# Unread transposes at the waits of block 1, step lists of their own for the first two units, and five instead of four leading pairs in block 3

## The chip, the cores and the metric

The kernel runs on one core of one Trainium2 chip. A core has five engines that run side by side, each with its own queue of instructions: PE (matrix products and transposes), DVE (vector operations), ACT (activation functions and copies), POOL (GpSimd, elementwise work here) and SP, which only issues transfers here. The metric is the device time of one execution in microseconds (us). A span in the profile begins with the first recorded instruction, and all positions below are microseconds from there.

PE has a clock that a throttle grants. The profile shows it as a share of full speed. In this trace it is either 1.00 or 0.50, and it changes only at the ends of windows of 3.413 us, so a position such as "the window 1002.41 to 1005.82" below means one of these.

## The reference, cut to what matters

The activations are 4 sequences of 256 tokens with 512 features, 1024 tokens in all. Two layers run one after the other, each made of a mixer and a feed-forward part, each with a layer norm ahead of it and a residual sum behind it:

```python
x = x + _L0_attn_ref(_layernorm(x), ...)   # block 1: retention, 32 heads of 128, 8 key/value heads
x = x + _L0_ffn_ref(_layernorm(x), ...)    # block 2: router, top 8 of 64, adds a mix of biases
x = x + _L1_attn_ref(_layernorm(x), ...)   # block 3: state space mixer, 128 heads of 64, 8 groups
x = x + _L1_ffn_ref(_layernorm(x), ...)    # block 4: top 16 of 64 low-rank adapters
```

Block 1, for each head and in chunks of 128 tokens:

```python
q = rope(h @ Wq.T); k = rope(h @ Wk.T); v = h @ Wv.T
G = cumsum(softplus(h @ Win.T + dt_bias) * -exp(A_log_bias))
scores = (q @ k.T) * where(causal, exp(G[i] - G[j]), 0)
y = scores @ (v * dt) + (carried state of the earlier chunk)
y = y / rms(y) * gnorm_w * silu(h @ Wg.T)
out = y @ Wo.T
```

Block 3 has the same shape with other parts: a projection to x, B and C, a causal convolution over 4 tokens with a silu behind it, products of C, B and a decay matrix for each head, a gate, an RMS norm within each of the 8 groups, and an output projection.

## The kernel before, in words

The tokens lie in 8 tiles of 128 (`k.x[0]` to `k.x[7]`), and are worked on in two halves of 4 tiles, which are 512 columns for PE. The normalised activations lie in `k.xs[half]` with features on the partitions, split into a rounded high part and the remainder: `xs_hi`, `xs_lo`. Every weight is split in the same way when it has been loaded (`split`, L140 on ACT for the high part, L145 on POOL for the low part), and a product is hi·hi + lo·hi + hi·lo. A projection (`proj`, L206) is thus 12 matmuls of 128x512, which take some 4.7 us at full clock.

`Weights` (L151 to L191) holds all weight pieces of the kernel in one list in order of use; a piece is 512 KB. `until(n)` splits all pieces up to the n-th and issues the loads of the next two; there are two raw buffers, so a load waits until the piece two places ahead has been split. `step` (W in the lists) splits one more piece if the position `due` allows; in block 1 `due` is -1, so W does nothing there. Pieces whose index is in `LATE` keep their place in program order on ACT. In all other things each engine's order is made by a scheduler from its own estimates of durations, under the dependencies and under extra order constraints: `k.line` fixes the order of PE instructions between steps, and `k.behind(a, b)` puts a behind b without a wait for data.

Block 1 (`retention`, L310 to L593) works in 32 units, each a key/value group, a pair of heads and a half. For each unit one of three lists of steps is followed: `FIRST1` for unit 0, `STEP1` for most, `SIDE1` while side work is pending. The letters: Q queries of the next unit (projection and rotation), K keys, values and transposed values of a next group, G gates (projection), S scores (L408, and L412 on DVE, which multiplies the decay matrix `m` with the scores), A attend and square (L420, L438), U silu, N the norm's transposes (L445) and the gate's product (L448), D decays of the next unit (L299 on POOL or DVE, L303, then exponentials), F and C the output projection of a unit (`finish`, L464, with the weight `wo`), P side work. One unit's `wo` is split by the first call of `u.w.o()`, that is in F, which stands in the next unit's list.

Ahead of unit 0 the layer norm of both halves runs tile by tile (`moments` L86 on DVE, a power on POOL, `centre` L101, transposes by `turned` L109, high part on ACT, low part L127 on DVE), mixed with the first keys, the time steps and the first gates.

Near the end of block 1, half 0's residual is finished before half 1's, and its share of the router (block 2) and of block 3's preparation begins as side work in the units that remain.

Block 3 (`state_space`, L672 to L980) works in 64 units: 8 groups by 4 head pairs by 2 halves. In the list `order` (L899) the first entry is a range whose pairs are all done for half 0 first and then for half 1; after that each pair is done for half 0 and at once for half 1, with the same weights in place; the last two pairs are again done half by half. Where two units of a pair don't follow each other, the weights (`wx`, `wg`, `wo`, and `wbc` for the first pair of a group) are loaded and split once for each half. With `FIRST3 = 1` and `NC = 8` the first range has 1·8//2 = 4 pairs, 0_0 to 0_3. Half 1 can start only once its residual, router and preparation are done; until then `while after.half not in ready` pumps side work, among it the running sums `ps_cum` (L255) that need `e` (L251).

Of the kernel before, what the change touches and what calls it, by code (L numbers as in the profile page):

```python
# [11 lines left out]
F32 = mybir.dt.float32  # L12
F32R = mybir.dt.float32r
AF = mybir.ActivationFunctionType
ALU = mybir.AluOpType
# [3 lines left out]
P = 128  # L19
NB, SEQ, HID = 4, 256, 512  # L20
NT = NB * SEQ // P
KC = HID // P
HT = NT // 2
# [1 line left out]
EPS = 1e-5  # L25
GONE = -30000.0
YB = 3
LONE1, FIRST3, LONE3 = 3, 1, 2
PUMP = 1
AHEAD = 0  # L30
BANK1, BANK3 = "o", "x"
LATE = (0, 3)
FIRST1 = "U S0 S1 S2 K Q0 W Q1 K A0 A1 W K G0 N0 W G1 N1 D E W".split()
STEP1 = "S0 D F S1 S2 K Q0 W Q1 K A0 A1 U W K C W P G0 N0 W G1 N1 E P W".split()
SIDE1 = "S0 D F P S1 S2 T K Q0 P W Q1 T K A0 A1 U W K C P P W G0 P N0 W G1 N1 E P W".split()
STEP3 = "W T0 T1 B I0 W M0 M1 X0 X1 I1 O0 G0 W W O1 W W P O2 W W G1 P W O3 D0 D1 W W".split()
FILL3 = "B X0 X1 I0 I1 P P G0 G1 W W P P W D0 D1 E E".split()
# [44 lines left out]
def moments(k, tc, t, tag):  # L82

    nc = tc.nc
    stats = k.small([P, 6], f"stats_{tag}_{t}", "ln_stats")
    nc.vector.bn_stats(stats, k.x[t])  # L86
    mv = k.small([P, 2], f"mv_{tag}_{t}", "ln_mv", 6)
    nc.vector.bn_aggr(mv, stats)
    rstd = k.small([P, 1], f"rstd_{tag}_{t}", "ln_rstd", 6)
    nc.gpsimd.tensor_scalar_add(rstd, mv[:, 1:2], EPS)  # L90
    one = nc.gpsimd.tensor_tensor(rstd, rstd, k.neghalf[:, 0:1], ALU.pow)
    if tag == "4" and t == HT - 1:
        k.rooted = one
    return mv[:, 0:1], rstd
# [10 lines left out]
def turned(k, tc, xn, name):  # L105

    ps = k.psum.tile([P, KC, P], F32, tag=k.bank, name=f"ps_{name}")
    for c in range(KC):
        k.line(tc.nc.tensor.transpose(ps[:, c, :], xn[:, c * P:(c + 1) * P], k.ident))  # L109
    return ps  # L110


def normalize(k, tc, half, tag, into=("xn",)):


    nc = tc.nc
    tiles = [HT * half + at for at in range(HT)]
    of = [moments(k, tc, t, tag) for t in tiles]
    ahead = len(into)
    xns = [centre(k, tc, tiles[at], of[at], tag, into[at]) for at in range(ahead)]  # L120
    yield
    for at, t in enumerate(tiles):
        xn = xns[at]
        ps = turned(k, tc, xn, f"xn_{tag}_{t}")
        hi, lo = (part[:, :, at * P:at * P + P] for part in k.xs[half])
        nc.scalar.copy(hi, ps)
        nc.vector.tensor_tensor(lo, ps, hi.bitcast(F32), ALU.subtract)  # L127
        if at + ahead < HT:
            xns.append(centre(k, tc, tiles[at + ahead], of[at + ahead], tag, into[at % ahead]))
        yield  # L130
# [179 lines left out]
def retention(k, tc, io, arrive, begun, done, tail):  # L310
# [3 lines left out]
    nc = tc.nc  # L314
    NH, NG = 32, 8
    with ExitStack() as st:
# [5 lines left out]
        n = 2 * NH * 2  # L322
# [29 lines left out]
        def rope(ps, hi, lo, name):  # L352
# [3 lines left out]
            if name == "k_0_0":  # L356

                tc.keep_in_program_order(one)
            t2 = k.wk.tile([P, 2, SEQ], F32, tag="xd", name=f"r2_{name}")
            nc.vector.tensor_tensor(t2[0:64], ps[64:128], mid(sin[64:128], 2), ALU.mult)  # L360
            nc.vector.tensor_tensor(t2[64:128], ps[0:64], mid(sin[0:64], 2), ALU.mult)  # L361
            nc.gpsimd.tensor_tensor(t1, t1, t2, ALU.add)  # L362
            t1 = t1.rearrange("p b s -> p (b s)")
            nc.scalar.copy(hi, t1)
            nc.vector.tensor_tensor(lo, t1, hi.bitcast(F32), ALU.subtract)

        def keys(g, half, w):

# [30 lines left out]
        def scores(u, blk):  # L399

            kh, kl = u.kk
            zj, zi = ((0, 0), (1, 1), (0, 1))[blk]
            ps = k.psum.tile([P, 4, P], F32, tag="y", name=f"ps_sc_{u.name}_{blk}")
            for b in range(2):
                aj = slice((2 * b + zj) * P, (2 * b + zj) * P + P)
                ai = slice((2 * b + zi) * P, (2 * b + zi) * P + P)
                for i, (a, q) in enumerate(((kh, 0), (kh, 1), (kl, 0))):
                    k.line(nc.tensor.matmul(  # L408
                        ps[:, b::2, :], a[:, aj], qs[:, q, :, ai], start=(i == 0), stop=(i == 2)
                    ))  # L410
            m = u.m[:, blk]
            nc.vector.tensor_tensor(m, m, ps, ALU.mult)  # L412

        def attend(u, z):
            blocks = (((0, 0),), ((0, 2), (1, 1)))[z]
            nm = f"{u.name}_{z}"
            ps = k.psum.tile([P, 4, P], F32, tag="g", name=f"ps_y1_{nm}")
            for q in range(4):
                for i, (zj, blk) in enumerate(blocks):
                    k.line(nc.tensor.matmul(  # L420
# [19 lines left out]
        def norm(u, z):  # L440

            nm = f"{u.name}_{z}"
            ps_t = k.psum.tile([P, 4, P], F32, tag="y", name=f"ps_yt1_{nm}")
            for q in range(4):
                k.line(nc.tensor.transpose(ps_t[:, q, :], u.yr[z][:, q, :], k.ident))  # L445
            r = k.wk.tile([P, 4, P], F32, tag="yh", name=f"r1_{nm}", bufs=YB)
# [62 lines left out]
        for i in range(-1, len(units) + 1):  # L509
# [50 lines left out]
            def value(z):  # L560
# [111 lines left out]
def state_space(k, tc, io):  # L672
# [461 lines left out]
def tile_two_layers(ctx: ExitStack, tc: tile.TileContext, io: dict, out: bass.AP):  # L1134
# [47 lines left out]
    def line(ins):  # L1182
# [5 lines left out]
        k.front = []  # L1188
        k.done = ins

    k.act, k.small, k.pump, k.behind, k.line = act, small, pump, order, line
    k.n, k.follow, k.done, k.main, k.root = 0, None, None, None, None
    k.rooted = None
    k.front = []
    k.hold = k.scaled = k.turned = None
    k.const = ctx.enter_context(tc.tile_pool(name="const", bufs=1))
    k.smalls = ctx.enter_context(tc.tile_pool(name="smalls", bufs=3))
    k.dram = ctx.enter_context(tc.tile_pool(name="dram", bufs=1, space=bass.MemoryType.DRAM))
# [110 lines left out]
```

## Time and profile before

| what | value |
|---|---|
| median of 3 runs | 2536.8 us (2534.87 to 2537.2) |
| the profiled execution | 2536.5 us, of which the span is 2534.7 us |
| mean granted clock of PE | 0.987 |
| PE busy | 2425.6 us, 96% of the span, 14000 matmuls and transposes |
| DVE, POOL, ACT busy | 2062.1, 1597.8, 1473.0 us (81%, 63%, 58%) |
| DMA | 206.25 MB, 81 GB/s on average |

The profiled execution is 0.3 us below the median of the runs, so a saving can be taken from the one or the other. The 36875 instructions of the trace are grouped by their line in the kernel. Durations are those of the records; in the slices of the page each digit is a share in tenths. In the views by window the columns are the stretch and its length, then busy time and number of instructions of PE, PE's weight loads, DVE, ACT and POOL, then the granted clock, the mean busy share of the DMA engines and GB/s. In the timelines the columns are start, duration, engine, line, operation, output and inputs, shape, the number of instructions taken together, and in brackets how long the engine stood idle ahead of it and what ended the wait. Idle time in PE sums to 109 us (2534.7 − 2425.6).

### The profile page before, as it was taken

The numbers are of one execution on the slowest core, as the hardware profiler recorded it, in microseconds if no ns is written. First come the engines' busy times: TensorE is split into PE (matmuls) and PEld (weight loads), VectorE is DVE, ScalarE is ACT, GpSimd is POOL, SyncE is SP. The second block draws the span as 40 slices with busy tenths as digits, with TensorE's granted clock in tenths as the row PEclk, the third lists the DMA queues.
The fourth block names the chain that finished last, engine by engine and source line by source line (L and its number), as shares of the span: only waits on it lengthen the run. The fifth ranks groups of instructions, "written<-read, shape, count | busy, mean of one in ns | idle before, by whom it ended". The sixth has DMA issues, their size and how long they took to land.

```text
span 2534.7 us, 36875 instructions
## 1 busy us (share of the span) xinstructions
PE 2425.6 (96%) x14000; PEld 2008.6 (79%) x14000; DVE 2062.1 (81%) x2629; ACT 1473.0 (58%) x2363; POOL 1597.8 (63%) x1123
## 2 busy tenths in 40 slices
PE   7899999999999897899999999999999999999989
PEld 6688888888887775678878888888888888888767
DVE  6577677778888769697988988988988988979973
ACT  3555555556655455465766756666756657657631
POOL 4555546557766547485874865856756855857840
PEclk9899999999999998999999999999999999999999
DMA  3312212213332222332232323222323223323221
GB/s 108 77 58 67 57 44 67 68 50 100 92 92 63 88 77 69 96 117 76 84 92 69 107 67 92 92 76 84 100 67 100 84 67 96 95 69 108 82 90 69
DMA packets 82896, 206.25 MB, mean 81 GB/s; under 512 B 8672, under 2 KB 10592, under 8 KB 82720
## 3 DMA queue, kind: packets, MB, share of 16 engines
q1 hardware_dynamic: 82720, 203.90, 26.5%
q8 instruction: 111, 1.82, 0.3%
q14 instruction: 65, 0.53, 0.1%
HBM read 200.86 MB, written 3.01 MB: 80 GB/s over the span
## 4 chain that ended last, share of the span: by engine, by line
PE 37%; DVE 15%; POOL 6%; issue 4%; ACT 3%; DMA 1%; POOLq 0%; SPq 0%; ACTq 0%; DVEq 0%
PE ps_x L206 9%; PE ps_g L206 8%; PE ps_o L877 8%; DVE m L773 4%; PE ps_y L821 4%; DVE conv L732 3%; PE ps_bc L206 3%; DVE yl L840 2%; PE ps_o L1122 2%; POOL xs L835 1%; DVE m L299 1%; POOL sqs L849 1%; PE ps_t L796 1%; PE ps_h L206 1%; ACT m L1160 1%
## 5 line engine op out<-in xcount | busy, mean ns | idle before, releaser
L206 PE MATMUL ps_g<-xs_hi,wg_h 128*128 128x512 f32 x768 | 306.4, 399 | 2.3 <-ACT wg_h L140 1.7
L773 DVE TENSOR_TENSOR m<-m,cb 128x1536 f32<-128x1536 f32 x128 | 274.7, 2150 | 40.2 <-ACT m L1160 38.8
L206 PE MATMUL ps_g<-xs_lo,wg_h 128*128 128x512 f32 x768 | 300.1, 391 | 0.0
L206 PE MATMUL ps_g<-xs_hi,wg_l 128*128 128x512 f32 x768 | 298.6, 391 | 0.0
L732 DVE SCALAR_TENSOR_TENSOR conv<-ps_x,cw,conv 128x510 f32<-128x510 f32 (+2 forms) x384 | 269.9, 736 | 20.1 <-ACT conv L730 17.5
L1157 ACT ACT_TABLE_LOAD x191 | 245.1, 1283 | 4.1 <-PEq L1297 0.8
L299 POOL TENSOR_TENSOR m<-gb,start 128x512 f32<-128x512 f32 x128 | 151.4, 1185 | 140.6 <-PE ps_y L821 93.0
L877 PE MATMUL ps_o<-wo_h,yh 128*128 128x512 f32 x512 | 213.0, 416 | 20.0 <-DVE acc L885 18.9
L835 POOL TENSOR_TENSOR xs<-xs,sg 128x512 f32<-128x512 f32 x128 | 206.7, 1615 | 38.2 <-DVE xs L831 37.3
L849 POOL TENSOR_TENSOR sqs<-sqs,sq 128x512 f32<-128x512 f32 x112 | 192.9, 1722 | 32.9 <-ACT sq L847 32.9
L362 POOL TENSOR_TENSOR r_q<-r_q,r_q 128x512 f32<-128x512 f32 x64 | 103.3, 1613 | 175.0 <-DVE r_q L361 174.8
L303 POOL TENSOR_SCALAR_AFFINE_SELECT m<-m 128x1024 f32<-128x1024 f32 x160 | 206.0, 1287 | 0.1
L877 PE MATMUL ps_o<-wo_h,yl 128*128 128x512 f32 x512 | 198.2, 401 | 7.8 <-DVE yl L840 7.8
L1160 ACT ACTIVATE xs<-conv,cb 128x512 f32<-128x512 f32 x128 | 90.8, 723 | 193.2 <-DVE conv L732 193.1
L877 PE MATMUL ps_o<-wo_l,yh 128*128 128x512 f32 x512 | 202.7, 396 | 0.0
L206 PE MATMUL ps_x<-xs_lo,wx_h 128*128 128x512 f32 x512 | 202.6, 396 | 0.0
L206 PE MATMUL ps_x<-xs_hi,wx_h 128*128 128x512 f32 x512 | 202.0, 395 | 0.4 <-DVE conv L732 0.2
L206 PE MATMUL ps_x<-xs_hi,wx_l 128*128 128x512 f32 x512 | 201.3, 393 | 0.0
L1160 ACT ACTIVATE m<-m 128x1024 f32<-128x1024 f32 (+1 forms) x160 | 181.5, 1135 | 28.0 <-POOL m L303 28.0
L145 POOL TENSOR_TENSOR wo_l<-raw_wo,wo_h 128x1024 fp32r<-128x1024 f32 x60 | 147.8, 2464 | 79.1 <-ACT wo_h L140 71.8
L145 POOL TENSOR_TENSOR wx_l<-raw_wx,wx_h 128x1024 fp32r<-128x1024 f32 x38 | 96.3, 2534 | 154.3 <-ACT wx_h L140 141.5
L821 PE MATMUL ps_y<-m,xd 128*64 128x128 f32 x2048 | 178.1, 280 | 13.5 <-DVE m L773 9.5
(276 smaller groups left out, 6949.1 us busy)
## 6 DMA issues: line engine op xcount, KB each, us to landing
gb<-cum SPq DMA_DIRECT2D x160, 512.0 KB
raw_wx<-in_L_attn_in_x_dram SPq DMA_DIRECT2D x38, 512.0 KB
raw_wg<-in_L_attn_in_gate_dram SPq DMA_DIRECT2D x38, 512.0 KB
raw_wo<-n_L_attn_out_proj_w_dram SPq DMA_DIRECT2D x38, 512.0 KB
raw_wq<-in_L_attn_Wq_dram SPq DMA_DIRECT2D x22, 512.0 KB
raw_wg<-in_L_attn_Wg_dram SPq DMA_DIRECT2D x22, 512.0 KB
raw_wo<-in_L_attn_Wo_dram SPq DMA_DIRECT2D x22, 512.0 KB
raw_wkv<-in_L_kv_dram SPq DMA_DIRECT2D x11, 512.0 KB
```

Source lines behind the costliest of these rows:

```text
L145: low = nc.gpsimd.tensor_tensor(lo, w, hi.bitcast(F32), ALU.subtract)
L206: k.line(tc.nc.tensor.matmul(ps, a[:, c, :], b[:, c, :], start=(c == 0 and n == 0), stop=(c == KC - 1 and n == 2)))
L299: one = engine.tensor_tensor(m[:, blk], gb[:, min(blk, 1)], last(at, P), ALU.add)
L303: nc.gpsimd.affine_select(out=causal, in_=causal, compare_op=ALU.is_ge, fill=GONE, base=0, pattern=[[0, 8], [1, P]], channel_multiplier=-1,)
L732: nc.vector.scalar_tensor_tensor(acc[:, :, j:], ps[:, :, :SEQ - j], cw[:, ch, TAPS - 1 - j:TAPS - j], acc[:, :, j:], ALU.mult, ALU.add,)
L773: made = nc.vector.tensor_tensor(mh, mh, cbs[p.g, p.half].rearrange("p z b l -> p z (b l)").unsqueeze(2) .to_broadcast([P, 3, 2, 2 * P]), ...
L821: one = nc.tensor.matmul(ps_y[h * D:h * D + D, 2 * b + z, :], p.xe[:, n, b, h, :] if blk == 2 else xd[:, 2 * b + zs, h, :], m[:, blk, 2 * ...
L835: nc.gpsimd.tensor_tensor(xs, xs, p.sg[n], ALU.mult)
L849: nc.gpsimd.tensor_tensor(total, total, sq, ALU.add)
L877: own.out = nc.tensor.matmul(ps, y[:, at], w[:, n, :], start=(i == 0), stop=(i == 5))
L1157: load = nc.scalar.preload_act_table_set(table)
L1160: ins = nc.scalar.activation(out, in_, func, bias=bias, scale=scale)
```

## The change: what it does

There are three edits.

First, `k.warm(n, ...)` issues n transposes of the identity into a tile of PSUM that nothing reads, at a fixed place in PE's order. There are 88: 14 behind the first score matmul of unit 0, 8 ahead of the third block of scores of unit 0 and 8 each ahead of the first and third of unit 1, 14 ahead of the transposes of `xn_3_3` (tile 3 of the layer norm of block 3, at the turn from block 1 to block 3), 18 ahead of the last unit's second attend, and 9 ahead of the norm of each of the last two units.

Second, order in block 1. `FIRST1` and `STEP1` lose entries W and get V: in unit 0, V splits all weight pieces up to that unit's `wo`; in unit 1 it splits up to the pieces of the second group's keys; in later units it does nothing. One more index, 7, is kept in program order. In the layer norm, half 1's statistics (`bn_stats`) of a tile are put behind half 0's low part of the tile with the same number ("half 0 first"), and the rotation of the second keys `k_0_1` behind the low part of the rotation before it ("queries first").

Third, `FIRST3` is 5 and counts pairs: half 0 runs 0_0 to 0_3 and 1_0, then half 1 runs the same five, and from 1_1 on each pair is done for both halves. Pair 1_0 is the first of group 1, so four more pieces (`wbc`, `wx`, `wg`, `wo`) are loaded and split once more: four transfers of 512 KB, four casts on ACT and four subtractions on POOL.

```diff
-LONE1, FIRST3, LONE3 = 3, 1, 2
+LONE1, FIRST3, LONE3 = 3, 5, 2
-LATE = (0, 3)
-FIRST1 = "U S0 S1 S2 K Q0 W Q1 K A0 A1 W K G0 N0 W G1 N1 D E W".split()
-STEP1 = "S0 D F S1 S2 K Q0 W Q1 K A0 A1 U W K C W P G0 N0 W G1 N1 E P W".split()
+LATE = (0, 3, 7)
+WARM = {"xn_3_3": 14}
+WARM1 = {(0, 2): ("g", 8), (1, 0): ("g", 8), (1, 2): ("g", 8)}
+FIRST1 = "U S0 S1 S2 K Q0 Q1 K A0 A1 K V G0 N0 G1 N1 D E".split()
+STEP1 = "S0 D F S1 S2 K Q0 W Q1 K A0 A1 V U K C P G0 V1 N0 G1 N1 E P".split()
...
-    nc.vector.bn_stats(stats, k.x[t])
+    one = nc.vector.bn_stats(stats, k.x[t])
+    if tag == "1" and t >= HT:
+        k.behind(one, k.parts[t - HT], "half 0 first")
...
+    if name in WARM:
+        k.warm(WARM[name], into=ps[:, KC - 1, :])
...
-        nc.vector.tensor_tensor(lo, ps, hi.bitcast(F32), ALU.subtract)
+        k.parts[t] = nc.vector.tensor_tensor(lo, ps, hi.bitcast(F32), ALU.subtract)
...
+            if name == "k_0_1":
+                k.behind(one, k.low, "queries first")
...
-            nc.vector.tensor_tensor(lo, t1, hi.bitcast(F32), ALU.subtract)
+            k.low = nc.vector.tensor_tensor(lo, t1, hi.bitcast(F32), ALU.subtract)
...
+            n = units.index(u)
+            if (n, blk) in WARM1:
+                k.warm(WARM1[n, blk][1], WARM1[n, blk][0])
...
+                    if (n, blk, b, i) == (0, 0, 0, 0):
+                        k.warm(14, "g")
...
+            if u is units[-1] and z == 1:
+                k.warm(18, into=ps[:, 3, :])
...
+            if u in units[-2:] and z == 0:
+                k.warm(9, into=ps_t[:, 3, :])
...
+                V=lambda n=0: k.weights.until(u.w.o.n if i == 0 else units[4].w.kv.n - 1 + n if i == 1 else -1),
...
-    order = [range(FIRST3 * NC // 2)]
+    order = [range(FIRST3)]
...
+    def warm(n, tag=None, into=None):
+        if into is None:
+            k.n += 1
+            into = k.psum.tile([P, P], F32, tag=tag, name=f"ps_warm_{k.n}")
+        if k.follow is None:
+            k.follow = k.done
+        for _ in range(n):
+            line(nc.tensor.transpose(into, k.ident, k.ident))
+        k.follow = k.done
```

More of the change, by code (lines that the diff above doesn't have):

```diff
@@ L1189, in line @@
         k.done = ins
+    def warm(n, tag=None, into=None):
[7 more added lines that the diff above has]
+        k.follow = k.done
     k.act, k.small, k.pump, k.behind, k.line = act, small, pump, order, line
+    k.warm = warm
     k.n, k.follow, k.done, k.main, k.root = 0, None, None, None, None
@@ L1195, in tile_two_layers @@
     k.hold = k.scaled = k.turned = None
+    k.parts = {}
     k.const = ctx.enter_context(tc.tile_pool(name="const", bufs=1))
```

## The prediction, made before the changed kernel ran

> **What bounds the kernel now.** I read the stretches by window first: busy time of PE, weight loads, DVE, ACT, POOL, then the clock.
>
> ```profile
> 60.00:80.00 20.00, 15.37 (x89) 12.54 (x87) 12.79 (x19) 11.20 (x28) 12.55 (x11) 0.93 0.33 88
> 80.00:100.00 20.00, 13.35 (x61) 10.86 (x62) 8.02 (x11) 10.44 (x10) 11.31 (x7) 0.72 0.48 127
> ...
> 1000.00:1050.00 50.00, 38.40 (x230) 29.36 (x230) 38.87 (x48) 20.99 (x31) 27.11 (x16) 0.90 0.26 79
> 1400.00:1800.00 400.00, 396.02 (x2459) 325.83 (x2457) 355.82 (x423) 261.41 (x361) 272.75 (x172) 1.00 0.28 85
> ```
>
> In steady block 3 PE is busy 396.02 of 400 us: PE is the bound, nothing is to be had there. The change works where PE idles and its clock falls: 4.6 of 20 us idle at 60 to 80, 6.65 at 80 to 100 with a clock of 0.72, 11.6 of 50 at 1000 to 1050. All of PE's idle time is 109 us. Next PE's timeline, for the waits at those places (in brackets the wait and what ended it).
>
> ```profile
> 53.62 0.58 PE L408 MATMUL ps_sc<-qs,kh 128*128 128x256 f32 x1 [3.71 <-DVE qs L365]
> 76.75 0.51 PE L408 MATMUL ps_sc<-qs,kh 128*128 128x256 f32 x2 [2.37 <-DVE r L448]
> 85.43 1.22 PE L464 MATMUL ps_o<-wo_h,yh 128*128 128x512 f32 x2 [7.54 <-ACT wo_h L140]
> 87.87 0.79 PE L464 MATMUL ps_o<-wo_l,yh 128*128 128x512 f32 x1 [1.22 <-POOL wo_l L145]
> ...
> 842.73 1.11 PE L109 MATMUL ps_xn<-ident,xn 128*128 128x128 f32 x4 [3.14 <-DVE xn L101]
> ...
> 892.24 2.95 PE L420 MATMUL ps_y<-v,m 128*128 128x128 f32 x16 [3.72 <-DVE m L412]
> ...
> 1033.12 2.08 PE L255 MATMUL ps_cum<-upper,e 128*128 128x128 f32 x8 [7.03 <-DVE e L251]
> ```
>
> The longest is for a weight. Its transfer was issued early and its cast came late:
>
> ```profile
> 21.48 0.33 SPq L176 DMA_DIRECT2D raw_wo<-in_L_attn_Wo_dram  x1
> ```
>
> ```profile
> 84.35 1.03 ACT L140 CAST wo_h<-raw_wo 128x1024 fp32r<-128x1024 f32 x1
> ```
>
> So this wait is one of order and not of data: the cast stands in the list of unit 1 and not in that of unit 0. The clock I read in its own windows of 3.41 us, first all of PE, then its transposes alone (those that read the identity).
>
> ```profile
> 1002.41:1005.82 3.41, 1.90 (x18) 1.25 (x14) 3.41 (x6) 1.69 (x2) 3.16 (x4) 1.00 0.44 154
> 1005.82:1009.23 3.41, 2.94 (x11) 2.04 (x10) 3.41 (x6) 3.40 (x7) 3.41 (x3) 0.50 0.00 0
> 1070.66:1074.07 3.41, 1.53 (x24) 1.32 (x24) 3.41 (x4) 3.38 (x5) 0.00 (x0) 1.00 0.56 179
> 1074.07:1077.48 3.41, 3.14 (x14) 2.61 (x15) 3.41 (x4) 3.17 (x5) 2.61 (x2) 1.00 0.33 125
> ```
>
> ```profile
> 1002.41:1005.82 3.41, 1.53 (x10) 1.00 0.44 154
> ```
>
> A window with 1.90 us of PE, 1.53 of it transposes, was followed by half clock; one with 1.53 us and no transpose kept full clock. The clock follows the matmuls, and transposes did not hold it.
>
> **The change part by part.** The profiled execution took 2536.5 us (span 2534.7), 0.3 under the median of 2536.8; the sum is made against 2536.5.
>
> (a) "Half 0 first". On DVE half 1's statistics stand between half 0's low parts: two of 0.69 us ahead of the second low part at 10.46. Put behind them, half 0's last tiles turn some 0.6 us earlier and the first time-step matmul comes at 13.5 and not 14.18: −0.7 (0 to −1.2). The order adds a wait for half 1's statistics: behind them stand their aggregates, POOL's powers and half 1's transposes, which nothing needs before the second time steps.
>
> (b) Unit 0. The second score matmul waits 3.71 us for the low part of the rotated queries; POOL's sum for it (1.6 us) stood behind two decay sums L299 (1.2 each), then came DVE's rotation of k_0_1 (2.1 us). The changed orders put the queries' sum ahead of L299 and that rotation behind. The low part is then ready at about 48.5 and PE at 48.9: the wait goes (−3.71), and with it the drop of the clock at 53.50 to 56.92, of which some 2.4 us are work at half speed (−1.2). The 14 transposes, at 0.0875 us each (4 transposes of the norm take 0.35 from start to start at full clock), now cost their 1.2. The 8 ahead of block 2 lie in the wait for the decays' exponentials, about 1 us. Sum −3.7 (−1.2 if a wait for the second product's other inputs stays, −4.9 if the 14 are covered). The rotation moved back feeds half 1's keys, first needed units later.
>
> (c) Unit 1. `wo`'s cast moves to about 66, behind the squares of unit 0, its subtraction on POOL to 69, into POOL's idle 4.37 us there. The waits of 7.54 and 1.22 go: −8.76. What is late next is `r` (L448): on DVE both decay sums L299, for units 1 and 2, now stand ahead of it, and they wait for their broadcast transfers gb (issued 68.52, landed 75.34). By the shift of (a) and (b) they land near 71, the scores come at 74.0 where the shift alone gives 72.35: +1.65. The third block's scores wait some 0.3 longer for L412. The 12 output matmuls stay at half clock. Sum −6.8 (−3.6 to −9.2: the upper end if the cast waits on ACT as long as the 2.37 us of the row above and the transfers don't come earlier, the lower if the clock holds). Queries of unit 2 start at 82.0 and not 93.17, −11.2 with (a) and (b). The pieces split earlier than before (V, V1) bring transfers and splits forward; POOL is busy 11 of 20 us here.
>
> (d) End of block 1. The 14, 18 and 9 transposes take 1.2, 1.6 and 0.8 us and lie inside waits of 3.14, 3.72, 2.04 and 1.47 us: 0 (up to +3 where such a wait has gone, since the earlier work brings them together). Their clock windows stay at half, by the reading above. Other orders there (the gate's product no longer behind a transfer wait of its queue) give −2, from one wait of 2.04 (0 to −4).
>
> (e) Block 3. Between the last value transposes of half 1's preparation and its running sums PE now has 46 matmuls ready at 0.228 us, 10.5 us, and before 24, 5.5. DVE's chain to `e` (1021.09 to 1033.07) gets three convolutions of 0.74 us between, so `e` comes at about 34.8, and the wait of 7.03 falls to 3.4: −3.6. At half 1's first pair PE waits 1.76 us for `m` and 0.53 for a gate's silu; both stages are now fed by a fifth pair: −2.3. Against that four more pieces: each 512 KB on SP's queue, a cast on ACT of 1.05, a subtraction on POOL of 2.5. DMA engines are 26% busy there, POOL 27 and ACT 21 of 50 us, so they lie beside PE's work; where one is late its user waits. No row shows these splits; the ends are 0 and 4 × 1.76 = 7, and I take +2, nearer to steady block 3, whose 1% idle holds such splits. Net −3.9 (−10, with all waits of the stage gone, to +4).
>
> Sum: −0.7 −3.7 −6.8 −2.0 −3.9 = −17.1: 2519.4, by the median 2519.7.
>
> **The rivals.**
>
> A: the transposes hold the clock. Then (c) runs its 12 output matmuls at full speed (−2.4), the stretch 841.98 to 848.81 its 5.4 us of work at twice the speed (−2.7), and 893.18 to 896.59 too (−1.7): −6.8, 2512.6. For it: waits are filled, and a filled PE otherwise kept its clock. Against it: the window at 1002.41. The Trainium skill, "TensorE: Matmul & The Clock Gate", section "Why this matters for your kernels", says that an idle gap of over some 3 us between bursts of matmuls loses the clock; read as a rule on any PE work it gives this rival. Its section "Part 4: PE-mode transpose" says that transposes don't count as such work; the window at 1002.41 agrees with that one.
>
> B: block 3's part gives nothing: −3.6 stays, the two short waits stay, four pieces cost 7: net +3.4, and the rest −13.2: 2526.7. For it: lone pairs reload all, and DVE is at 3.41 of 3.41 us in both quoted stretches, so `e` can come as late as PE's new work is long. Against it: PE had 11.6 us idle there.
>
> C, slower: the pieces of the fifth pair are split when they are needed, as `wo` was at 84.35, so cast, subtraction and the wait behind lie on the path: 1.05 + 2.5 + 1.76 = 5.3 us, by 4 21.2, 2536.5 − 13.2 + 21.2 = 2544.5. It decides from 13.2 us. For it: it happened in unit 1. Against it: in block 3 W splits ahead of need, and PE idles 1% there.
>
> D: V does not do what it says, and the cast of `wo` stays late: without (c), 2526.2. The cast is an order on ACT that a scheduler decides; in the changed program it stands ahead of unit 1's scores.
>
> **How the numbers follow.** A difference under 0.2%, 5 us, is about what a measurement of this kernel can't tell from none. Chances: the forecast 0.52 (its own range 2513 to 2525), A 0.12, B 0.17, D 0.04; block 3 losing between 8 and 18 us, so that nothing is left, 0.06; C 0.09. Faster 0.85, same 0.06, slower 0.09. The range goes from A with the lower ends of (c) and (d), 2505, to B with the upper ends of (b) and (d), 2531, and leaves out 0.15.
>
> **What would show it.** (a) first time-step matmul at 13.5; (b) no wait of over 1 us before the second score matmul and full clock until about 70; (c) cast of `wo` before 70, queries of unit 2 near 82; (d) the 14 and 18 transposes inside waits that end as before, half clock behind them; (e) the wait for `e` at 3 to 4 us, and no wait of over 2 us for wbc, wx, wg, wo of 1_0. I am wrong if DVE, which now carries more between 60 and 80 and at 1020, becomes what PE waits for, or if the clock falls at new places.

## The result, and the profile after

The changed kernel took 2520.9 us (median of 6 runs, 2515.6 to 2522.3) against 2536.5 of the kernel before: a ratio of 0.9936 with an interval of 0.9923 to 0.9949. A second set on another occasion gave 2519.0 us and 0.9926 (0.9914 to 0.9939). It is faster, by 16 to 17 us; 2519.4 had been forecast (2519.7 by the median). One of the six runs of the kernel with four leading pairs, which is used below, took 4917 us and is left out of its median. The profiled executions are 2536.5 and 2519.2 us, 17.3 apart, and the sum of the prediction was 17.1. The total came out, but the stages show that it did so by terms that missed on both sides.

To compare stages, both traces are cut at the same piece of PE's work: the first matmul of the queries of units 1, 2 and 31 (Q1, Q2, Q31), the first B and C projection of block 3 (BC0), the first time-step projection for its half 1 (DT1), the first B and C projection of group 2 and group 7 (BC2, BC7), the first matmul of the two routing products of block 4 (R0, R1), and the end.

| stage, us | before | after | difference | predicted |
|---|---|---|---|---|
| start to Q1 | 57.6 | 57.6 | +0.1 | −4.4 (a, b) |
| Q1 to Q2 | 35.6 | 26.3 | −9.3 | −6.8 (c) |
| Q2 to Q31 | 760.5 | 761.4 | +0.9 | 0 |
| Q31 to BC0 | 20.9 | 21.3 | +0.4 | (d) |
| BC0 to DT1 | 137.0 | 125.1 | −11.9 | −2.0 (d) |
| DT1 to BC2 | 296.8 | 293.0 | −3.8 | −3.9 (e) |
| BC2 to BC7 | 904.1 | 904.5 | +0.4 | 0 |
| BC7 to R0 | 215.8 | 218.2 | +2.4 | 0 |
| R0 to R1 | 33.5 | 40.4 | +6.9 | 0 |
| R1 to the end | 72.9 | 69.6 | −3.4 | 0 |

How far a stage moves from one execution to the next was seen in a second profiled execution of the changed kernel: Q1 to Q2 was 28.2 there and not 26.3, all others were within 1.1 us. (Other kernels with one and the same order in a stage differ by more in one case, DT1 to BC2, as will be seen.)

The windows that were shown of before, now of after (stretch, length, busy time of PE, weight loads, DVE, ACT, POOL, then clock, DMA share, GB/s):

```profile
60.00:80.00 20.00, 18.44 (x108) 15.24 (x107) 14.16 (x21) 13.57 (x30) 16.47 (x13) 1.00 0.44 128
80.00:100.00 20.00, 18.99 (x108) 16.37 (x107) 13.50 (x19) 12.44 (x26) 13.47 (x13) 1.00 0.23 64
1000.00:1050.00 50.00, 46.97 (x291) 38.24 (x290) 37.95 (x50) 28.79 (x40) 31.81 (x18) 1.00 0.37 105
1400.00:1800.00 400.00, 397.06 (x2473) 327.53 (x2472) 357.47 (x428) 260.88 (x359) 276.95 (x173) 1.00 0.28 85
```

PE is nearly full at 60 to 100 and the clock is 1.00 there; steady block 3 is what it was. PE's waits in the changed kernel, by its timeline (line numbers are those of the changed kernel: L420 is L408 of before, L482 is L464, L466 is L448):

```profile
48.80 1.69 PE L1218 MATMUL ps_warm<-ident 128*128 128x128 f32 x14
51.70 0.38 PE L420 MATMUL ps_sc<-qs,kh 128*128 128x256 f32 x1 [1.21 <-DVE qs L374]
...
56.82 0.50 PE L420 MATMUL ps_sc<-qs,kh 128*128 128x256 f32 x2 [2.23 <-DVE m L426]
...
76.64 0.50 PE L420 MATMUL ps_sc<-qs,kh 128*128 128x256 f32 x2 [1.40 <-DVE r L466]
...
833.58 0.66 PE L116 MATMUL ps_xn<-ident,xn 128*128 128x128 f32 x4 [1.63 <-DVE xn L106]
...
878.65 2.13 PE L1218 MATMUL ps_y<-ident 128*128 128x128 f32 x18
...
1033.84 0.50 PE L896 MATMUL ps_o<-wo_h,yh 128*128 128x512 f32 x1 [2.02 <-ACT yh L858]
...
1191.18 0.69 PE L840 MATMUL ps_y<-m,xd 128*64 128x128 f32 x4 [4.16 <-DVE m L792]
...
2412.59 0.80 PE L213 MATMUL ps_lg<-xs_lo,wr_parts 128*128 128x512 f32 x1 [4.35 <-DVE xs_lo L134]
```

The waits of 7.54 for `wo_h`, 7.03 for `e` and 3.72 for `m` are gone. Three of over 2.1 us are new: 2.23 us at 56.82, on the decays' products; 4.16 us at 1191.18, on block 3's product of the decays with those of C and B, with half clock from 1189.7 to 1196.5; and 4.35 us at 2412.59, on a low part in block 4, far from every edit. What DVE did ahead of the product that PE waits for at 1191.18:

```profile
1181.25 8.12 DVE L910 SCALAR_TENSOR_TENSOR x<-acc,r,x 128x512 f32<-128x512 f32 x4 [2.24 <-POOL r L882]
```

Four residual sums wait 2.24 us for POOL there and end at 1189.37. In the two kernels with four leading pairs DVE's timeline lists no wait ahead of the same four sums, and PE has no wait of over 1 us behind them; in all twelve profiles with five leading pairs PE waits 4.0 to 4.9 us. The cast of `wo` in ACT's timeline stands where the prediction put it, a little later:

```profile
69.29 1.05 ACT L147 CAST wo_h<-raw_wo 128x1024 fp32r<-128x1024 f32 x1
```

### The profile page after: what moved, and what is told of

It is laid out like the page before. It is cut to its first block, busy times and chain, and to the rows that moved or that the text cites. A ratio compares the mean times of both kernels' runs of the same rounds, so it can differ in the third digit from the quotient of the medians.

```text
span 2517.4 us, 37059 instructions
## 1 busy us (share of the span) xinstructions
PE 2430.5 (97%) x14088; PEld 2015.1 (80%) x14088; DVE 2067.6 (82%) x2629; ACT 1476.6 (59%) x2367; POOL 1603.9 (64%) x1127
## 4 chain that ended last, share of the span: by engine, by line
PE 58%; DVE 23%; POOL 8%; ACT 5%; issue 4%; DMA 2%; SPq 0%; POOLq 0%; ACTq 0%; DVEq 0%
PE ps_g L213 11%; PE ps_x L213 7%; PE ps_o L896 7%; PE ps_q L213 6%; PE ps_o L482 6%; DVE conv L751 5%; DVE m L792 5%; PE ps_y L840 3%; PE ps_bc L213 2%; PE ps_sc L420 2%; DVE yl L859 2%; PE ps_y L436 2%; DVE m L306 2%; PE ps_o L1141 2%; ACT m L1179 2%
## 5 line engine op out<-in xcount | busy, mean ns | idle before, releaser
L306 POOL TENSOR_TENSOR m<-gb,start 128x512 f32<-128x512 f32 x128 | 149.5, 1171 | 133.2 <-PE ps_y L840 98.0
L152 POOL TENSOR_TENSOR wo_l<-raw_wo,wo_h 128x1024 fp32r<-128x1024 f32 x61 | 152.8, 2505 | 68.8 <-ACT wo_h L147 67.0
L840 PE MATMUL ps_y<-m,xd 128*64 128x128 f32 x2048 | 178.4, 280 | 14.7 <-DVE m L792 14.1
```

The lines of the kernel that those rows point to most:

```text
L152: low = nc.gpsimd.tensor_tensor(lo, w, hi.bitcast(F32), ALU.subtract)
L306: one = engine.tensor_tensor(m[:, blk], gb[:, min(blk, 1)], last(at, P), ALU.add)
L840: one = nc.tensor.matmul(ps_y[h * D:h * D + D, 2 * b + z, :], p.xe[:, n, b, h, :] if blk == 2 else xd[:, 2 * b + zs, h, :], m[:, blk, 2 * ...
```

## The experiments

All kernels are timed against the kernel before. "Stage" means the cuts of the table above, in one profiled execution each.

**No transposes at all.**

```diff
     def warm(n, tag=None, into=None):
+        if k.follow is None:
+            k.follow = k.done
+        return
```

> The changed kernel without its 88 transposes that nothing reads; all else, also the order of the steps, as in the changed kernel. Stages by the trace of the changed kernel: from the second unit's queries to the third's 26.3 us, from the last unit's queries to the third group's B and C 439.5 us, from the first to the second routing product of block 4 40.4 us. Theory 1, the recorded one (transposes do not hold the clock): the clock stays where it is in the changed kernel, also from 19 to 92 us, the first of these stages stays within 0.5 us of 26.3, the second too. Theory 2 (transposes hold the clock): the clock falls to half near 53 and near 74 us, the first stage is 2 to 4 us longer, and near 880 us, where the 18 and the 9 stood, a window falls as well, 1 to 2 us. Both: here the order on DVE in block 4 has the last low part of half 0 ahead of the four residual sums, as in the kernel before, so the stage of block 4 should go from 40.4 back to 33.5 us, about -7. In all: theory 1 about 2513, theory 2 about 2517 to 2519.

Measured: 2536.1 us, ratio 0.9994 (0.9985 to 1.0004). Without the 88 transposes the whole change is worth nothing. Neither theory had that. Half clock came back at 52.8 to 63.0 and 80.1 to 83.5, and Q1 to Q2 took 28.6 us, as theory 2 said, and R0 to R1 went back to 34.2. But the large loss was elsewhere: BC0 to DT1 took 137.7 and not 125.1 us, although only 27 of the transposes stand in that stage, all in its first 20 us (in the changed kernel 18 at 878.65 and 9 at 885.17). The orders of the two programs show why that can be: without the transposes the scheduler puts DVE, ACT, POOL and PE into another order from the end of block 1 into block 3. The transposes are all that was taken out.

**Four leading pairs.**

```diff
-LONE1, FIRST3, LONE3 = 3, 5, 2
+LONE1, FIRST3, LONE3 = 3, 4, 2
```

> The changed kernel with four leading pairs in block 3, as before. The recorded prediction puts the fifth pair at -3.9 us, so the stage from the last unit's queries to the third group's B and C goes from 439.5 to about 443.5 us. The rival, read from the two traces (this stage fell by 15.2 us in all): the fifth pair is worth 8 to 14 us, and the stage comes out at 448 to 453 with the wait of about 7 us for e back. In both the order on DVE in block 4 is again that of the kernel before, so the block 4 stage goes from 40.4 to about 33.5. In all: prediction about 2516, rival 2521 to 2526.

Measured: 2515.8 us (median of five runs), 0.9913 (0.9895 to 0.9931). DT1 to BC2 is 296.1 and not 293.0: the fifth pair is worth 3.1 us in its own stage in this pair of executions, near the 3.9 predicted, and the rival of 8 to 14 falls. BC0 to DT1 is 125.3, so the large gain there isn't the fifth pair's. And R0 to R1 is 33.1, BC7 to the end 321.7 where the changed kernel has 328.1: the kernel with four pairs is not slower as a whole, because the changed kernel loses 6.4 us in block 4.

**The lists of before.**

```diff
-LATE = (0, 3, 7)
+LATE = (0, 3)
-FIRST1 = "U S0 S1 S2 K Q0 Q1 K A0 A1 K V G0 N0 G1 N1 D E".split()
-STEP1 = "S0 D F S1 S2 K Q0 W Q1 K A0 A1 V U K C P G0 V1 N0 G1 N1 E P".split()
+FIRST1 = "U S0 S1 S2 K Q0 W Q1 K A0 A1 W K G0 N0 W G1 N1 D E W".split()
+STEP1 = "S0 D F S1 S2 K Q0 W Q1 K A0 A1 U W K C W P G0 N0 W G1 N1 E P W".split()
```

> The changed kernel with the step lists of block 1 and the kept places of the kernel before (no V, wo of unit 0 is split in unit 1's list). Recorded prediction: V is worth 6.8 us, and the wait of about 7.5 us before the first output product comes back, so the stage from the second unit's queries to the third's goes from 26.3 to about 33. Rival: V is worth all of the 9.3 us that this stage gained, 35.6. If the transposes hold the clock through the wait it ends nearer 33 with full clock at 80 us, if not nearer 36 with half clock. Block 3 and block 4 as in the changed kernel: 2526 to 2529 in all.

Measured: 2528.8 us, 0.9968 (0.9957 to 0.9980). Q1 to Q2 is 35.1 us, 8.8 more, and the wait is back, with half clock from 79.5 to 89.7; PE's timeline of this run:

```profile
83.59 1.22 PE L482 MATMUL ps_o<-wo_h,yh 128*128 128x512 f32 x2 [7.72 <-ACT wo_h L147]
86.02 0.80 PE L482 MATMUL ps_o<-wo_l,yh 128*128 128x512 f32 x1 [1.21 <-POOL wo_l L152]
```

So the lists carry nearly all of (c); the 8 transposes ahead of the scores (at 73.94) don't bridge a wait of that length.

**The low part ahead of the residual sums in block 4.**

```diff
         if (p.g, p.half) == (NG - 1, 0):
             k.behind(one, own.made, "products first")
+        if (p.g, p.half) == (NG - 1, 1):
+            k.behind(one, k.parts[HT - 1], "low part first")
```

> The changed kernel with one more order on DVE: in block 4 the four residual sums of half 1 stand behind the last low part of half 0's layer norm, as they do by chance in the kernel before. Theory: this order alone cost the changed kernel the 4.35 us wait before the second routing product and the half clock behind it, so the stage between the two routing products goes from 40.4 to about 33.5 us, and the time to about 2513. Rival: the sums that move back make half 1 later by as much, the end gains less than 2 us: 2518 to 2520.

Measured: 2514.5 us, 0.9911 (0.9897 to 0.9926); R0 to R1 is 35.4 and not 40.4. DVE in the changed kernel:

```profile
2407.07 4.86 DVE L910 SCALAR_TENSOR_TENSOR x<-acc,r,x 128x512 f32<-128x512 f32 x4 [1.13 <-POOL r L882]
2411.86 0.68 DVE L134 TENSOR_TENSOR xs_lo<-ps_xn,xs_hi 128x512 fp32r<-128x512 f32 x1
```

and with the added order:

```profile
2407.53 0.69 DVE L134 TENSOR_TENSOR xs_lo<-ps_xn,xs_hi 128x512 fp32r<-128x512 f32 x1 [1.81 <-ACT xs_hi L133]
2408.13 3.88 DVE L910 SCALAR_TENSOR_TENSOR x<-acc,r,x 128x512 f32<-128x512 f32 x4
```

Four sums that wait 1.13 us for POOL and then run 4.86 us stood ahead of the one low part that PE needed. In the kernel before the low part came first (at 2427.07, the sums at 2429.78). The order was the scheduler's, not the edit's.

**Early transposes out.**

```diff
-WARM1 = {(0, 2): ("g", 8), (1, 0): ("g", 8), (1, 2): ("g", 8)}
+WARM1 = {}
-                    if (n, blk, b, i) == (0, 0, 0, 0):
-                        k.warm(14, "g")
```

> The changed kernel without the 14 and the three times 8 unread transposes of units 0 and 1; the 41 at the end of block 1 stay, and up to about 835 us every engine's order is that of the changed kernel. Theory 2 (transposes hold the clock): half clock appears between 50 and 90 us, as in the kernel without any of the 88, and the stage from the second unit's queries to the third's is 28 to 29 us where the changed kernel has 26.3. Theory 1 (they do not): no half clock there, 26.3 us or a little less. The stage from the last unit's queries to the third group's B and C should stay near 439.5 us, since its transposes are in place; should it go to 455, the early ones act through the schedule of what comes later.

Measured: 2518.7 us, 0.9937 (0.9922 to 0.9952), no difference to the changed kernel that can be told. Half clock did appear, from 54.6 to 61.4, and the third unit's queries begin at 86.7 us, against 83.9 and 86.4 in the two executions of the changed kernel; Q1 to Q2 is 27.2, short of what theory 2 expected. Over all runs, the third unit's queries begin at 86.7 and 87.2 us in the two kernels without these transposes (this one and the first experiment) and at 83.9 to 86.4, mean 85.2, in seven executions with them and an otherwise equal front: 1 to 2 us, which the total is too coarse to show. It isn't there any more where the last unit's queries begin: Q31 is at 845.4 us in this run, and at 845.4 and 846.9 in the two executions of the changed kernel.

**Late transposes out, and the orders pinned.** Three runs separate the transposes from the order that they bring about. First the 41 at the end of block 1 are left out and the scheduler is free:

```diff
-WARM = {"xn_3_3": 14}
+WARM = {}
...
-            if u is units[-1] and z == 1:
-                k.warm(18, into=ps[:, 3, :])
...
-            if u in units[-2:] and z == 0:
-                k.warm(9, into=ps_t[:, 3, :])
```

> The changed kernel without the 41 unread transposes at the end of block 1 (14, 18, 9, 9); the scheduler, which counts them in its own timeline, then also orders the engines in another way from the end of block 1 into block 3. The stage from the last unit's queries to the third group's B and C was 439.5 us with all 88 and 456.4 with none, so about 455 is expected by every theory; if it stays at 440, the early 38 were the cause.

Then, for the two others, each engine's instructions from there into block 3 are chained in a given order, without waits for data (`PINS` lists their places; `late_off` with the places of the changed kernel, the changed kernel with the places of `late_off`):

```diff
+def pin(k, tc):
+    ...
+    for engine, runs in PINS.items():
+        for run in runs:
+            for first, then in zip(run, run[1:]):
+                tc.add_manual_dep(
+                    by[engine][then], by[engine][first].name,
+                    mybir.DependencyInfo(mybir.DependencyClass.NoSync, mybir.DependencyReason.DATA),
+                    reason="pinned",
+                )
...
         of.run4()
+        pin(k, tc)
```

> No transposes at the end of block 1, as in the run above, but PE, DVE, ACT, POOL and SP are pinned to the order that they have in the changed kernel from there into block 3. Theory A (the transposes' gain there is an accident of the schedule: they move the scheduler's estimates, and it orders DVE, ACT and POOL better): the stage stays at 439 to 442 us. Theory B (they hold PE's clock, or fill it, in the waits): about 452 to 456 us.

> The counterpart: the changed kernel with all its transposes, but all engines from the end of block 1 into block 3 pinned to the order that the scheduler makes when the 41 are not there. Theory A: the stage from the last unit's queries to the third group's B and C is 453 to 457 us although the transposes are in place. Theory B: 438 to 443 us.

| | order of the changed kernel | order made without the 41 |
|---|---|---|
| with the 41 transposes | 2520.9 us; BC0 to DT1 125.1 | 2526.0 us (0.9960); BC0 to DT1 136.0 |
| without them | 2520.3 us (0.9934); BC0 to DT1 123.2 | 2532.5 us (0.9986); BC0 to DT1 137.1 |

From Q31 to BC2, the stage of the expectations, it is 439.5 and 455.4 us in the first row and 438.8 and 452.4 in the second: theory A. The stage follows the column, not the row: the order is worth 11 to 14 us from BC0 to DT1, the transposes by themselves nothing there. By their traces the two kernels of a column have the same order on PE, DVE, ACT and POOL from Q31 to BC2. (The totals of the first row differ by less, since pinning also gave block 4 another order: R0 to R1 is 31.4 us in the upper right kernel and 40.4 in the changed one.) The windows from BC0 to DT1, with the transposes but the other order, and then without them in the changed kernel's order:

```profile
864.82:1000.84 136.02, 117.34 (x672) 93.48 (x670) 105.80 (x154) 72.21 (x114) 80.85 (x69) 0.95 0.29 89
```

```profile
869.11:992.33 123.22, 112.43 (x643) 89.36 (x642) 98.28 (x153) 72.83 (x114) 79.24 (x68) 0.97 0.30 94
```

PE's idle time falls from 18.7 to 10.8 us, and its half clock from 13.7 to 6.8. Which wait goes is seen in PE's timeline with the transposes and the other order,

```profile
950.43 0.70 PE L840 MATMUL ps_y<-m,xd 128*64 128x128 f32 x4 [2.80 <-DVE xe L826]
973.19 0.79 PE L896 MATMUL ps_o<-wo_h,yh 128*128 128x512 f32 x1 [4.81 <-DVE acc L904]
```

and what DVE did ahead of the second of them:

```profile
968.61 3.92 DVE L680 TENSOR_SCALAR x<-x,by 128x512 f32<-128x512 f32 x4 [2.04 <-POOL by L678]
972.46 1.27 DVE L904 TENSOR_TENSOR acc<-acc,ps_o 128x512 f32<-128x512 f32 x2
```

Four steps of the router wait 2.04 us for POOL and run 3.92 us, ahead of the sum whose PSUM buffer PE waits for; the kernel before has the same two lines and both of PE's waits:

```profile
979.31 3.92 DVE L661 TENSOR_SCALAR x<-x,by 128x512 f32<-128x512 f32 x4 [2.04 <-POOL by L659]
983.16 1.27 DVE L885 TENSOR_TENSOR acc<-acc,ps_o 128x512 f32<-128x512 f32 x2
```

```profile
961.13 0.44 PE L821 MATMUL ps_y<-m,xd 128*64 128x128 f32 x4 [2.81 <-DVE xe L807]
983.89 0.80 PE L877 MATMUL ps_o<-wo_h,yh 128*128 128x512 f32 x1 [5.21 <-DVE acc L885]
```

In the changed kernel the four steps stand earlier (86.8 us behind BC0, against 103.8 in the upper right kernel), wait 0.41 us, and PE's longest wait of the stage is 1.83 us:

```profile
953.49 2.89 DVE L680 TENSOR_SCALAR x<-x,by 128x512 f32<-128x512 f32 x4 [0.41 <-POOL by L678]
```

PE's longest wait of this stage is 1.8 us in all nine profiles with the good order, that of the pinned kernel without the 41 among them, and 4.1 to 5.5 us in the five with the other. PE's own order differs between the two as well, so how much of the gain is DVE's order alone isn't separated.

The two kernels in the left column also give a clean pair for the clock, since they differ in the transposes alone. The clock windows at the first norm of the last two units, in the changed kernel (9 unread transposes in the first one),

```profile
858.60:862.02 3.42, 2.35 (x17) 1.91 (x16) 3.42 (x7) 3.39 (x6) 0.54 (x1) 1.00 0.01 2
862.02:865.43 3.41, 3.41 (x21) 2.91 (x20) 2.72 (x4) 2.11 (x8) 2.96 (x2) 1.00 0.00 0
```

and in its order without them:

```profile
859.09:862.50 3.41, 1.39 (x7) 0.81 (x5) 3.41 (x8) 3.38 (x6) 0.93 (x1) 1.00 0.06 24
862.50:865.91 3.41, 3.38 (x10) 2.89 (x11) 2.72 (x4) 2.40 (x7) 2.57 (x2) 0.50 0.00 0
```

With them 2.35 us of PE, of which 1.50 are transposes, and the clock stays; without them 1.39 us, and the next window is granted half. In all three variants of the changed kernel without the 41 a window falls here; in none of the nine profiles with them does one. Q31 to BC0 takes 22.5 to 22.9 us in the three and 20.9 to 21.3 in the nine. (Of the two profiles in the order of before, also without them, a window falls in one, which takes 22.5 us; in the other, the kernel before, the clock fell later, at 893, and it takes 20.9.) So the transposes hold the clock, and here that is worth 1.2 to 2 us; at the end of the next two stages nothing of it is left (Q31 to BC2 is 439.5 us with them and 438.8 without).

The fourteen profiles together say how much work a window needs. Cut into the windows at whose ends the clock changes, and with the transposes counted as PE's work, each of the 88 windows at full clock with less than 1.4 us of PE was followed by half clock. Of about 100 with 1.4 to 2.0 us a third were, of some 9800 with more only 7. Windows whose work is transposes for four fifths or more lie on the same line: all nine with 0.3 to 1.35 us lost the clock, and of fourteen with 1.45 to 1.9 us thirteen kept it. So a transpose counts for the clock much as a matmul does.

**Without the two orders on DVE.**

```diff
-    if tag == "1" and t >= HT:
-        k.behind(one, k.parts[t - HT], "half 0 first")
...
-            if name == "k_0_1":
-                k.behind(one, k.low, "queries first")
```

> The changed kernel without the two extra orders on DVE ('half 0 first' and 'queries first'). Recorded prediction: the first is worth 0.7 us, the second 3.7, so unit 1's queries start 4.4 us later, near 62 us. Rival, from the trace of the changed kernel (57.64 us there, 57.56 before): the wait for the low part of the queries became a wait of 2.23 us for the product of decays and scores, whose exponentials now come at 52.71 and not 50.36; the orders are worth nothing, and unit 1's queries start within 1 us of 57.6, the time is 2519 to 2522.

Measured: 2519.0 us, 0.9927 (0.9913 to 0.9941); Q1 at 58.8 us, against 57.6 and 58.2 in the changed kernel. The two orders are worth nothing that can be told. PE's wait before the second score matmul is 2.18 us here, the one before the third block of scores isn't there.

**Five pairs alone, in the kernel before.**

```diff
-LONE1, FIRST3, LONE3 = 3, 1, 2
+LONE1, FIRST3, LONE3 = 3, 5, 2
...
-    order = [range(FIRST3 * NC // 2)]
+    order = [range(FIRST3)]
```

> The kernel before with five leading pairs in block 3 and nothing else; up to about 1020 us all orders are those of the kernel before. Recorded prediction for this part: -3.9 us, all of it between half 1's preparation and the third group's B and C (296.8 us before, 293.0 in the changed kernel). Rival, from the kernel with four pairs, which is faster than the changed one as a whole: the gain of about 3 us there is real, and it is given back if the scheduler puts the residual sums of half 1 ahead of the last low part in block 4. Here that low part stands one place behind where it stood before, but not behind the sums, so block 4 should not lose more than 1 us: 2533 to 2535 in all.

Measured: 2542.3 us, 1.0017 (1.0007 to 1.0027): slower than before, and not 2533 to 2535. DT1 to BC2 is 294.1, 2.7 less, so the gain in its own stage is there again. BC7 to the end is 325.6 against 322.2, a loss of 3.4 and not of at most 1. The two don't make the 6 us of the medians; another 4 us lie ahead of BC0 (878.6 against 874.6), where the orders are those of before. Of these, 1.0 is there at the first time-step matmul (15.2 us against 14.2), and 1.6 lies from Q31 to BC0, where a window at 872.4 fell. Why the rest is lost is not settled; the ten runs lie between 2532.1 and 2545.4.

How sure is the gain of about 3 us in the stage? Over all profiles DT1 to BC2 took 292.1 to 294.1 us in nine with five leading pairs, but 296.2, 296.6 and 298.5 in three others, and 296.8 and 296.1 in the two with four. Eight of the twelve have exactly the same order on PE, DVE, ACT and POOL there, and these alone took 292.7 to 298.5: the upper right kernel of the table above 298.5 and the one below it, in the same order, 292.8. So the mean gain is 2.3 us, and a single pair of executions can't show it.

**The exponentials first.** On top of the low part ahead of the sums, a pinned order in unit 0 (here as the places are exchanged):

```diff
 ACT
+exponentials of m, unit 0
 exponential of e, half 1
-cast of wq, unit 1
 vT copy
-exponentials of m, unit 0
+cast of wq, unit 1
 DVE
+m <- m, scores of block 0
+m <- m, scores of block 1
 room <- e (softplus, half 1)
 e <- room, e (softplus, half 1)
-m <- m, scores of block 0
-m <- m, scores of block 1
```

> The kernel with the low part ahead of the residual sums in block 4, and, in unit 0 of block 1, the exponentials of the decays put ahead of the time step's exponential and the cast of the next query weight on ACT, and the first two products of decays and scores ahead of two steps of the softplus on DVE (POOL changes one place, the second keys' sum ahead of a weight's low part). All other orders as there. If the exponentials are what took the place of the removed wait, the wait of 2.2 us before the third block of scores falls under 0.5 and unit 1's queries start at 55.5 to 56.5 instead of 57.6 to 58.3, and the time is 2511 to 2513. If PE then waits for something else there, such as the second keys or values, nothing is gained: 2514.

Measured: 2513.0 us, 0.9901 (0.9886 to 0.9917), the lowest of all, though its interval overlaps that of the kernel that it was built on (0.9897 to 0.9926); the changed kernel, timed beside it, gave 0.9926. Q1 is at 55.2 us, and at 58.3 in the kernel that it was built on. The third block of scores, which waited 2.23 us in the changed kernel, waits for nothing that the timeline lists:

```profile
54.38 0.50 PE L420 MATMUL ps_sc<-qs,kh 128*128 128x256 f32 x2
```

**The changed kernel again.**

> The changed kernel once more, on the same chip and in the same call as the kernel with the two further orders, so that the two can be held against each other. All theories: 2519 to 2522 us, ratio to the kernel before 0.992 to 0.995. The profile of this second execution also shows how far the stages differ from one execution to the next: under 1.5 us each.

Measured: 2519.0 us, 0.9926 (0.9914 to 0.9939). One stage, Q1 to Q2, differs by 1.9 us from the first execution, more than expected; the rest is within 1.1.

## Why the prediction was right as a sum and wrong in its parts

- **(a), −0.7.** The first time-step matmul came at 13.6 us in one execution of the changed kernel and at 14.1 in the other (before: 14.2). The kernel without the order has 14.4. The other kernels with the order have 13.6 to 14.5. A gain of 0.2 to 0.8 is possible, none is shown. (The second low part of before, which the term speaks of, stands at 11.65; the one at 10.46 is the first.)
- **(b), −3.7: wrong, in two steps.** The half clock at 53.50 went, as predicted (in two of the six other profiles with the same front a window fell at 57.0 all the same). The first step that failed is "the low part is then ready at about 48.5". POOL's sum moved ahead as predicted, but on DVE a decay sum and a step of the softplus (1.14 us at 49.91) came ahead of that low part, and it was ready at 51.65:

```profile
48.15 1.52 DVE L306 TENSOR_TENSOR m<-gb,room 128x512 f32<-128x512 f32 x1
...
50.97 0.68 DVE L374 TENSOR_TENSOR qs<-r_q,qs 128x512 fp32r<-128x512 f32 x1
```

So PE's wait did not go: the 14 transposes filled 1.69 us of it, and 1.21 were left. The second step is "the 8 ahead of block 2 lie in the wait for the decays' exponentials, about 1 us". The exponentials came at 52.71 and not 50.36, since POOL's mask of the decays moved from 48.77 to 49.81 (it needs DVE's own decay sum, L299 or here L306, which now stood behind the first low part, at 48.15 and not 46.61), and ACT took another exponential, a cast and a copy first. The wait was passed on: 2.23 us at 56.82. Moving the exponentials forward gave back 2.4 to 3.1 us, which shows that most of the gain had gone here.
- **(c), −6.8: right, undersized.** The trace has −9.3 (−7.4 in the second execution), the run with the old lists 8.8. The cast came at 69.29, not 66, and queries of unit 2 began at 83.9 and 86.4, not 82.0. What was missed is the clock: the 12 output products ran at full speed, where half had been assumed (the lower end of its range). They took 3.1 us from start to end, 77.44 to 80.56. (The 4.7 us given for the 12 matmuls of a projection are their durations added, which overlap; at full clock one starts every 0.23 us.)
- **(d), −2.0: the largest miss.** The gain was 11.9 us and it lay in the next stage, BC0 to DT1. The term was read as "other orders there", from one wait of 2.04 us. The waits of 2.8 and 5.2 us at 961 and 984 stand in the trace of before, 60 to 85 us behind the last edit of block 1, and the term left them out; the step that failed is that orders were weighed only around the edits. Nor did "their clock windows stay at half" hold: with the 18 and the two 9 in place no window fell from 858 to 890.
- **(e), −3.9: right in size, by other terms, so in part by luck.** −3.8 in the trace, 3.1 by undoing it, 2.7 by doing it alone, and 2.3 on the mean of all profiles. The wait for `e` went altogether (−7.0) and not to 3.4 (by the term's own figures, 5.0 us more of PE's work and `e` 1.7 later, it would be 3.7). The four more weight pieces, put at +2, show no wait of over 2 us. What took back the rest is the wait of 4.16 us at 1191.18, behind four sums on DVE that wait for POOL. As an edit the fifth pair gained nothing in the totals: 2520.9 and 2519.0 us with it against 2515.8 without, and 2542.3 against 2536.2 in the kernel before.
- **Missing from the sum: block 4, +5.9** (BC7 to the end). It was given no term. With four leading pairs it isn't there (321.7 us, before 322.2). The added order took back 5 us in its stage and 4.5 to 6.5 in the total (2514.5 against 2519.0 and 2520.9).
- **Rival A (the transposes hold the clock): right in kind, wrong in its price.** The reading that transposes did not hold the clock rested on one window with 1.90 us of PE, and windows of 1.4 to 2.0 us went both ways, those of matmuls alone too (of about 50 a third lost the clock); in the changed kernel a window with 1.53 us of PE, of which 1.47 were transposes, kept it (53.06 to 56.47), the count over all traces puts transposes and matmuls on one line, and the pair above differs in the transposes alone. The price of 6.8 us was too high: 1.2 to 2 at the end of block 1, 1 to 2 at the front, and the stretch behind the 14 (834.7 to 841.5) stayed at half clock in the first execution and for one window in the second. The Trainium skill, "TensorE: Matmul & The Clock Gate", section "Part 4: PE-mode transpose", says that the full clock doesn't engage for transposes, since they don't count as PE's busy time in the same way; this pair of windows and the count over all traces disagree, for keeping the clock, and the measurement decides. What decides between 1.4 and 2.0 us isn't settled.
- **Rival B and C: fell.** The wait for `e`, which B keeps, is gone in all twelve profiles with five leading pairs; C's 21 us for pieces split too late are in none. **Rival D: fell**, the cast moved. (The lower end of the range, A with the lower ends of (c) and (d), is 2508 by its own terms and not 2505, and it counts the full clock of the 12 output products twice.)

So −4.4 that did not come and +5.9 that was not foreseen were covered by 9.9 us more in (d) and 2.5 more in (c). That the total came out within 2 us was luck: the misses happened to cancel.

## What to carry to other kernels

Where a scheduler orders the engines from its own estimates, an edit acts in two ways, through what it does and through how it shifts every order behind it; here the second was the larger one, with 11 to 14 us gained behind the edits of block 1 and 6 lost in block 4, which no edit touches. Compare the orders of the two programs on every engine, not only around the edit, and look on DVE for runs of instructions that wait for a slow producer ahead of the one that PE waits for (three times here four steps that wait for POOL, with PE idle for 4.81, 4.16 and 4.35 us); pin the good order, since it can be lost with the next edit. And when a wait is taken away by putting something first, cost what is now second: a wait of 3.71 us became 1.69 us of transposes, a wait of 1.21 and one of 2.23.

## What the runs showed of the hardware

A transpose that nothing reads can keep PE's clock: nine of them in a window made 2.35 us of work out of 1.39 and saved the half clock behind it. It bridges a wait of 1 to 2 us within one window; with 8 transposes ahead of a wait of 7.72 us the clock fell all the same. In these traces a window of 3.41 us with less than 1.4 us of PE always lost the clock and one with over 2.0 us hardly ever (7 of some 9800). So it matters where the windows lie, which differs by execution. With all 14 transposes at 830 us in one window (1.78 to 1.81 us of PE, three profiles) the clock stayed; with only a part of them in it (1.31 us, the first execution of the changed kernel) the next 6.8 us were at half. Over the nine profiles with these 14 the half clock behind them was 0 to 6.8 us, over the five without them 6.8 in each.
